# Masking and row maxima of a cross-attention block: one fused VectorE operation per head in place of an add and a maximum per bank

## The chip, the cores and the metric

The kernel runs on one core of a Trainium2 chip. Five engines work side by side, each with its own queue of instructions that it runs in order: TensorE (PE in the profile; PEld is its loading of weights), VectorE (DVE), ScalarE (ACT), GpSimd (POOL) and SyncE (SP, which issues most of the transfers). They wait for one another through semaphores. PE writes to the eight banks of PSUM, each 128 partitions by 512 fp32 columns; the other data lie in SBUF. The metric is the device time of one execution in microseconds (us).

## What is computed

A cross-attention block over 128 batch entries of 128 positions and 256 features, with 16 heads of 16 features. Queries come from `x`, keys and values from the context; position i may look at positions j < i only; the softmax runs over j; row 0 is set to zero. Then follow the output product, a residual and a layer norm, a feed-forward part of 1024 with ReLU, and a second residual and norm.

```
scores = jnp.einsum('bhqd,bhkd->bhqk', q, k) / jnp.sqrt(jnp.float32(D_K))
scores = jnp.where(j < i + mask, scores, NEG_INF)      # mask = 0
attn = jax.nn.softmax(scores, axis=-1).at[:, :, 0, :].set(0.0)
ctx = jnp.einsum('bhqk,bhkd->bhqd', attn, v)
x = layer_norm(query + ctx @ Wo + bo, ln1_g, ln1_b)
out = layer_norm(x + jax.nn.relu(x @ W1 + b1) @ W2 + b2, ln2_g, ln2_b)
```

## The kernel before

Two batch entries make a pair p, so there are 64 pairs, 0 to 63. The pairs are worked on in an overlapped way: in step p the scores and the softmax are those of pair p, the weighing with the values those of pair p-2, the hidden layer that of p-3, the second product that of p-4, and the projections prepare pair p+1. Steps 7 to 62 are regular: each consists of the same operations, and the order in which each engine gets them is written out by hand. For the middle steps that is the string `ORDER` (L1746), whose words are looked up in the table `OPS` (L1642) and called by `step` (L1761); the first regular steps and the last one have their words in calls of `do` written out one by one. An entry such as `w1-1` belongs to the step before. The pairs outside 7 to 62 use other functions (`mask`, `mask_high`, `maximum`, `low_maximum`), which stay as they are.

Because of the causal mask the query rows are split in halves. For the low rows (the first 64 positions of both entries, laid over 128 partitions) only 64 key columns matter; for the high rows 128. `scores_both` (matmuls at L440) writes the high scores of four heads to each of the banks 0 to 3 and the low scores of four heads to each of the banks 4 to 7. The constant `neg` holds 64 zeros and then a triangle with -1e30 above the diagonal.

Then, in the order of DVE's queue in a regular step: `maskA0` adds the triangle to the low scores of heads 0 to 3 and writes SBUF (tile `sm`, L464); `add3` adds it in place, in PSUM, to the second 64 columns of heads 12 to 15 (`mask_add`, L1552); `maskA1` (heads 4 to 7, L464) and `maskB` (heads 8 to 15, L456) do the rest of the low ones; `max3` takes the negated maxima of the high heads 12 to 15 out of bank 3 (`mask_max`, L1558); `lowmax` takes those of all 16 low heads out of `sm` (L920). `add1`, `max1`, `add2`, `max2`, `add0` and `max0` follow further down the step, between other work.

ACT makes the exponentials, one head at a time, with the sum over the row as a second result (`exponential_by_head`, L931): exp(score + nmx), where `nmx` is the negated maximum. `eh7` (high heads 14 and 15) is the first of a step, `el7` (low heads 14 and 15) the last. The high exponentials read PSUM, the low ones `sm`; both write `sm`. Three transposes on DVE (L533, `turn1`, `turn0`, `turn2`) take `sm` to `turned`, and transfers on SP's queue bring it to `brought` for the weighing two steps later.

The banks are shared. After the scores PE goes on with `v1` (a product for the values, bank 4), `o1` (output product, bank 5) and `q1` (queries, bank 7), all at L1147; they overwrite the banks of the low scores. `w1` (second product) uses bank 6, `k1` (keys) bank 3, and the products of the hidden layer (L1358) banks 0 to 2. The context (L612 and L617 on DVE) multiplies the weighed values by the inverse sums and stands in DVE's queue right before `maskA0`; it waits for the weighing on PE (L586, L596), which is the last that PE does before the scores. Between its products PE runs a few no-ops that are written into the order too.

Of the kernel before, what the change touches and what calls it, by code (L numbers as in the profile page):

```python
# [9 lines left out]
AF = mybir.ActivationFunctionType  # L10
ALU = mybir.AluOpType
AX = mybir.AxisListType

P = 128
NEG_INF = -1e30
# [4 lines left out]
def tile_cross_attention_block(  # L20
# [22 lines left out]
    nc = tc.nc  # L43
    B, S, D = x.shape
# [10 lines left out]
    HP = P // 2  # L55
# [18 lines left out]
    states = {}  # L74
# [103 lines left out]
    neg = const.tile([P, 2, HP], F32, tag="neg", name="neg")  # L178
# [67 lines left out]
    banks = psum.tile([P, 8, 512], F32, tag="banks", name="banks")  # L246
# [202 lines left out]
    def mask(p, hi, rs):  # L449
        st = states[p]  # L450
        n = P if hi else HP
        no = neg.rearrange("p u j -> p (u j)") if hi else neg[:, 1, :]
        if not hi and len(rs) == 2 and rs[0] and "both" in st:
            r = rs[0]
            at = 4 + r
            nc.vector.tensor_tensor(  # L456
                st["sm", 0][:, 4 * r : 4 * r + 8, :].rearrange("p (b n) j -> p b n j", b=2),
                banks[:, at : at + 2, : 4 * n].rearrange("p b (n j) -> p b n j", j=n),
                no[:, None, None, :].to_broadcast([P, 2, 4, n]),
                ALU.add,  # L460
            )
            return
        for r in rs:
            nc.vector.tensor_tensor(  # L464
                st["sm", hi][:, 4 * r : 4 * r + 4, :],
                st["sps", hi][r][:, : 4 * n].rearrange("p (n j) -> p n j", j=n),
                no[:, None, :].to_broadcast([P, 4, n]),
                ALU.add,
            )
# [448 lines left out]
    def low_maximum(p):  # L918
        st = states[p]
        nc.vector.tensor_reduce(st["nmx", 0], st["sm", 0], AX.X, ALU.max, negate=True)  # L920

    def exponential_by_head(p, hi, heads, summed=False):

        st = states[p]
        if summed and "su" not in st:
            st["su"] = small.tile([P, 2 * H], F32, tag="su", name=f"su_{p}")
        sm, nmx = st["sm", hi], st["nmx", hi]
        for h in heads:
            at = h % 4 // 2 * H + hi * HH + h // 4 * 2 + h % 2
            src = st["sps", 1][h // 4][:, h % 4 * P : h % 4 * P + P] if hi else sm[:, h, :]  # L930
            nc.scalar.activation(sm[:, h, :], src, AF.Exp, bias=nmx[:, h : h + 1], scale=1.0, **(  # L931
                {"accum_out": st["su"][:, at : at + 1]} if summed else {}
            ))

    hidden_all = const.tile([P, FC, TP], F32, tag="hT", name="hT")
    wt = const.tile([P, 4, FC // 2, P], F32, tag="wt", name="wt")
# [189 lines left out]
    class Seven:  # L1126
# [28 lines left out]
        b = property(lambda self: self.of(1))  # L1155
        f = property(lambda self: self.of(2))
# [270 lines left out]
    for which, first in (("c", c_first[:, 0:2]), ("x", tokens_of[0][:, 0:2])):  # L1427
        st = states[0]
# [27 lines left out]
    for m in range(KC):  # L1456
# [7 lines left out]
        for e in range(2):  # L1464
            if m == 0:
                nc.scalar.activation(
                    st["kT"][:, m, e, :], pk[:, :TP], AF.Identity,
                    bias=bkh[:, m, e : e + 1], scale=half[:, e : e + 1],
# [9 lines left out]
    for m in range(KC):  # L1478
# [7 lines left out]
        if m == 0:  # L1486
            nc.scalar.activation(
                st["qT"][:, m, :], pq[:, :TP], AF.Identity,
                bias=bqs_c[:, m : m + 1], scale=QSCALE,
# [8 lines left out]
    A, B = (0, 1), (2, 3)  # L1498
# [47 lines left out]
        }[n]  # L1546
        engine.tensor_tensor(c[:, n], left, right, how)  # L1547

    def mask_add(p, b):

        ps = banks[:, b].rearrange("p (n j) -> p n j", j=P)
        nc.vector.tensor_tensor(  # L1552
            ps[:, :, HP:], ps[:, :, HP:], neg[:, 1, None, :].to_broadcast([P, 4, HP]), ALU.add
        )

    def mask_max(p, b):

        nc.vector.tensor_reduce(  # L1558
            states[p]["nmx", 1][:, 4 * b : 4 * b + 4],
            banks[:, b].rearrange("p (n j) -> p n j", j=P), AX.X, ALU.max, negate=True,  # L1560
        )

    KINDS = {
        "V": (Values, 4), "O": (Attention, 5), "Q": (Queries, 7), "K": (Keys, 3),
# [16 lines left out]
    def means_of(p):  # L1581

        st = states[p]
        mv = st["mva"] = small.tile([P, 4, 2], F32, tag="mv", name=f"mv_{p}")
        bs = st.pop(("bs", p))
        for s in range(4):
            nc.vector.bn_aggr(mv[:, s], bs[:, s])
# [25 lines left out]
    def turn_x1_blocks(p):  # L1613
        nc.vector.transpose(
            x1_turned(p).rearrange("p j (u a) -> p u j a", a=32),
            states[p]["x1"].rearrange("p s (k j a) -> p (s k) j a", k=KC, a=32),
        )
# [20 lines left out]
    def bring_part(p, n):  # L1638
# [3 lines left out]
    OPS = {  # L1642
        "weigh": lambda p: weigh(p - 2),
        "scores": lambda p: scores_both(p),
        "context": lambda p: context(p - 2),
        "deviations": lambda p: scales_of(p),
        "means": lambda p: means_of(p),
        "stats1": lambda p: stats_of(p, p - 2, "t1", 0),
        "stats2": lambda p: stats_of(p, p - 6, "t2", 2),
        "norm1": lambda p: norm1(p - 2),  # L1650
# [2 lines left out]
        "finish2": lambda p: finish_shift(p - 6),  # L1653
        "store": lambda p: store(p - 6),
        "turnx": lambda p: turn_x1_blocks(p - 2),
        "maskA0": lambda p: mask(p, 0, (0,)),
        "maskA1": lambda p: mask(p, 0, (1,)),
        "maskB": lambda p: mask(p, 0, B),
        "lowmax": lambda p: low_maximum(p),
        "recip": lambda p: reciprocals(p),  # L1660
        "turni": lambda p: turn_inverse(p),
        "load": lambda p: load_ahead(p),
# [75 lines left out]
            p + 2, "xc", halves(states[p + 2]["xT"]), n  # L1738
        ) if p + 2 < NP else None
    for n in range(HH):  # L1740
        OPS[f"eh{n}"] = lambda p, n=n: exponential_by_head(p, 1, (2 * n, 2 * n + 1), True)
        OPS[f"el{n}"] = lambda p, n=n: exponential_by_head(p, 0, (2 * n, 2 * n + 1), True)
    for n in range(3):
        OPS[f"turn{n}"] = lambda p, n=n: turn(p, n < 2, n % 2)

# [1347 lines left out]
```

## Time and profile before

| | us |
|---|---|
| runs of the kernel | 1475.64, 1478.79, 1478.85 (median 1478.79) |
| span of the profiled execution, whose own time the page gives only as this span | 1476.0 |
| busy: PE / DVE / ACT / POOL over the span | 1450.0 / 1372.8 / 1304.3 / 1266.4 |
| one regular step (612 to 634 us is one) | 22.03 |
| exponentials on ACT: high, 944 of them, mean | 0.383 |
| exponentials on ACT: low, 944 of them, mean | 0.369 |

In the profile a row of a view in order of time gives start, duration, engine, line, operation, result and sources, and in brackets the idle time in front with what ended it. A row of a group gives line, engine, operation, names, shapes and count, then the busy time, the mean duration in ns, and the idle time in front with the releasers. A row of a table by stretches gives the stretch, its length, the busy time and count of each engine, the clock that PE was granted (1.00 is full), the share of the transfer engines and GB/s.

### The profile page before, as it was taken

How to read it: one execution, taken by the hardware profiler on the slowest of the kernel's cores; microseconds unless marked ns; L12 is line 12 of the kernel's file. 1: busy time of each engine (PE TensorE's matmuls, PEld its weight loads, DVE VectorE, ACT ScalarE, POOL GpSimd, SP SyncE). 2: the span in 40 equal slices, each digit the busy share in tenths (PEclk: the TensorE clock that was granted, in tenths of full speed). 3: DMA queues.
4: the chain of work that ended last, by engine and by line, in shares of the span. 5: the costliest groups of instructions: out<-in, count | busy, mean ns of one | idle time of the engine just before them, and what ended most of it. 6: DMA issues, size and time to landing. Idle time of an engine off the chain costs nothing.

```text
span 1476.0 us, 61938 instructions
## 1 busy us (share of the span) xinstructions
PE 1450.0 (98%) x20713; PEld 1394.3 (94%) x20713; DVE 1372.8 (93%) x3231; ACT 1304.3 (88%) x5559; POOL 1266.4 (86%) x1816
## 2 busy tenths in 40 slices
PE   8999899999999999999999999999999999999998
PEld 7778799999999999999999999999999999999988
DVE  6987999999999999999999999999999999999767
ACT  4659899999999999999999999999999999999743
POOL 5986898988988988988988988888898888887966
PEclk9999999999999999999999999999999999999999
DMA  8274766766766767776766766766776766774541
GB/s 202 66 142 104 178 162 149 159 152 156 167 158 155 154 152 157 169 159 152 165 147 151 166 157 157 163 149 153 163 160 157 161 147 154 163 163 113 130 109 51
DMA packets 367448, 220.33 MB, mean 149 GB/s; under 512 B 279600, under 2 KB 335152, under 8 KB 367152
## 3 DMA queue, kind: packets, MB, share of 16 engines
q1 hardware_dynamic: 364864, 214.27, 63.9%
q8 instruction: 187, 3.06, 0.9%
q10 hardware_dynamic: 2288, 2.11, 0.7%
q14 instruction: 109, 0.89, 0.2%
HBM read 55.06 MB, written 18.09 MB: 50 GB/s over the span
## 4 chain that ended last, share of the span: by engine, by line
PE 72%; ACT 7%; DVE 4%; DMA 3%; SPq 1%; POOL 1%; issue 1%; DVEq 0%; ACTq 0%; POOLq 0%
PE banks L1147 40%; PE banks L1358 20%; PE banks L440 5%; ACT sm L931 5%; PE banks L596 3%; DMA kT<-kr 2%; PE banks L586 2%; PE banks L971 1%; DMA brought<-turned 1%; ACT kr L1213 1%; PE banks L869 0%; PE banks L1044 0%; ACT qT L1175 0%; SPq L552 0%; PE banks L629 0%
## 5 line engine op out<-in xcount | busy, mean ns | idle before, releaser
L931 ACT ACTIVATE sm<-banks,nmx 128x128 f32<-128x128 f32 x944 | 336.8, 383 | 15.8 <-DVE nmx L1558 12.6
L931 ACT ACTIVATE sm<-sm,nmx 128x64 f32<-128x64 f32 x944 | 321.6, 369 | 1.4 <-DVE nmx L920 1.4
L533 DVE STREAM_TRANSPOSE turned<-sm 128x1024 f32<-128x1024 f32 x186 | 217.0, 1213 | 3.3 <-DMA brought<-turned 2.4
L931 ACT ACTIVATION_READ_ACCUMULATOR sm<-banks,nmx 128x1 f32 x944 | 211.4, 224 | 0.0
L931 ACT ACTIVATION_READ_ACCUMULATOR sm<-sm,nmx 128x1 f32 x944 | 207.8, 220 | 0.0
L1147 PE MATMUL banks<-wt,hS 128*128 128x128 f32 x1344 | 177.6, 275 | 0.0
L1358 PE MATMUL banks<-xS,w1t 128*128 128x128 f32 x1344 | 177.2, 275 | 0.0
L1147 PEld LDWEIGHTS banks<-wt,hS 128*128 128x128 f32 x1344 | 163.6, 192 | 0.1
L1358 PEld LDWEIGHTS banks<-xS,w1t 128*128 128x128 f32 x1344 | 163.4, 192 | 0.0
L1558 DVE TENSOR_REDUCE nmx<-banks 128x4 f32<-128x512 f32 x224 | 152.1, 679 | 1.9
L1547 POOL TENSOR_TENSOR hS<-hT 128x512 f32<-128x512 f32 x116 | 147.5, 1273 | 5.4 <-ACT hT L876 2.4
L1358 PE MATMUL banks<-brought,w 128*128 128x128 f32 x896 | 118.2, 275 | 0.0
L1608 POOL TENSOR_TENSOR x1b<-x,g_r 128x512 f32<-128x512 f32 x56 | 72.3, 1291 | 51.0 <-ACT x L703 51.0
L1147 PE MATMUL banks<-w,hT 128*128 128x128 f32 x896 | 109.8, 275 | 0.0
L1358 PEld LDWEIGHTS banks<-brought,w 128*128 128x128 f32 x896 | 109.0, 192 | 0.0
L440 PE MATMUL banks<-kT,qT 32*64 32x128 f32 (+1 forms) x3840 | 100.7, 331 | 6.3 <-DMA kT<-kr 3.7
L1147 PEld LDWEIGHTS banks<-w,hT 128*128 128x128 f32 x896 | 104.8, 192 | 0.1
L440 PEld LDWEIGHTS banks<-kT,qT 32*64 32x64 f32 x3840 | 82.7, 131 | 16.9 <-ACT hT L1399 4.9
L1534 POOL TENSOR_TENSOR oc<-cxT 128x128 f32<-128x128 f32 x112 | 49.0, 457 | 57.9 <-DVE cxT L617 56.9
L1387 ACT ACTIVATE hT<-hT,b1e_c 128x256 f32<-128x256 f32 x224 | 95.7, 509 | 1.2 <-DVE hT L1383 1.1
L1552 DVE TENSOR_TENSOR banks<-banks,neg 128x256 f32<-128x256 f32 x224 | 93.1, 416 | 0.0
L703 ACT ACTIVATE x<-t,nb,sd 128x256 f32<-128x256 f32 x126 | 68.4, 592 | 19.1 <-POOL nb L726 11.9
(322 smaller groups left out, 4841.1 us busy)
## 6 DMA issues: line engine op xcount, KB each, us to landing
brought<-turned SPq DMA_DIRECT2D x936, 128.0 KB, 2.4
out_dram<-t SPq DMA_DIRECT2D x63, 256.0 KB, 4.7
xb<-in_x_dram SPq DMA_DIRECT2D x124, 128.0 KB, 3.2
cb<-in_ctx_dram SPq DMA_DIRECT2D x124, 128.0 KB, 3.2
x<-in_x_dram SPq DMA_DIRECT2D x31, 512.0 KB, 5.4
kT<-kr SPq DMA_DIRECT2D x112, 128.0 KB, 2.7
brought<-turned SPq DMA_DIRECT2D x40, 96.0 KB, 2.2
w<-in_L_xattn_W_dram SPq DMA_DIRECT2D x2, 1024.0 KB, 7.8
```

Of the source, the lines that this page charges most:

```text
L440: nc.tensor.matmul(st["sps", hi][r][s * HP : (s + 1) * HP, m * 2 * n : (m + 1) * 2 * n].rearrange("p (e j) -> p e j", e=2), st["qT"][strip ...
L533: nc.vector.transpose(turned[:, :, at : at + 256].rearrange("p j (n a) -> p n j a", a=32), states[p]["sm", hi].rearrange("p h j -> p (h j) ...
L703: nc.scalar.activation(x1[:, s], t1[:, s], AF.Identity, bias=st["nb", 1][:, s], scale=sd[:, s])
L931: nc.scalar.activation(sm[:, h, :], src, AF.Exp, bias=nmx[:, h : h + 1], scale=1.0, **({"accum_out": st["su"][:, at : at + 1]} if summed e ...
L1147: nc.tensor.matmul(out, left(k) if self.depth > 1 else left, right(k) if self.depth > 1 else right, start=(n == 1 and k == 0), stop=(k == ...
L1358: nc.tensor.matmul(ps[:, i * P : (i + 1) * P].rearrange("p (n a) -> p n a", a=32), left(i), right, start=(n in (1, 2, 5) and i == 0), stop ...
L1387: nc.scalar.activation(self.hT[:, f, at], self.hT[:, f, at] if src is None else src, AF.Relu, bias=b1e_c[:, f : f + 1], scale=1.0,)
L1534: nc.gpsimd.tensor_tensor(c[:, n], left, right, how)
L1547: engine.tensor_tensor(c[:, n], left, right, how)
L1552: nc.vector.tensor_tensor(ps[:, :, HP:], ps[:, :, HP:], neg[:, 1, None, :].to_broadcast([P, 4, HP]), ALU.add)
L1558: nc.vector.tensor_reduce(states[p]["nmx", 1][:, 4 * b : 4 * b + 4], banks[:, b].rearrange("p (n j) -> p n j", j=P), AX.X, ALU.max, negate ...
L1608: nc.gpsimd.tensor_tensor(st["x1b"], st["x1b"] if n else st["x1"], (be1b_r if n else g1_r)[:, None, :].to_broadcast([P, 2, D]), ALU.add if ...
```

## The change

In the regular steps each head gets one DVE operation that adds the mask, multiplies by -1 and takes the minimum over the row: it reads the scores from PSUM and `neg` from SBUF, writes the negated masked scores to `sm`, and gives the minimum (the negated maximum) as a second result into `nmx`. The exponentials of these steps then read `sm` for both halves, with the factor -1 and `nmx` as before. The words of the order stay where they are: `maskA0`, `maskA1` and `maskB` do the low heads 0 to 3, 4 to 7 and 8 to 15; `lowmax` does nothing; `add`n does the first two high heads of bank n and `max`n the other two. All other steps keep their masks.

```
-    def exponential_by_head(p, hi, heads, summed=False):
+    def exponential_by_head(p, hi, heads, summed=False, negated=False):
...
-            nc.scalar.activation(sm[:, h, :], src, AF.Exp, bias=nmx[:, h : h + 1], scale=1.0, **(
-                {"accum_out": st["su"][:, at : at + 1]} if summed else {}
-            ))
+            if negated:
+                src = sm[:, h, :]
+            nc.scalar.activation(
+                sm[:, h, :], src, AF.Exp, bias=nmx[:, h : h + 1], scale=-1.0 if negated else 1.0,
+                **({"accum_out": st["su"][:, at : at + 1]} if summed else {}),
+            )
...
+    def negated(p, hi, h):
+
+        st = states[p]
+        n = P if hi else HP
+        no = neg.rearrange("p u j -> p (u j)") if hi else neg[:, 1, :]
+        nc.vector.tensor_tensor_reduce(
+            st["sm", hi][:, h, :], st["sps", hi][h // 4][:, h % 4 * n : h % 4 * n + n], no,
+            -1.0, -2 * NEG_INF, ALU.add, ALU.min, st["nmx", hi][:, h : h + 1],
+        )
+
+    def low_negated(p, heads):
+        for h in heads:
+            negated(p, 0, h)
+
     def mask_add(p, b):
-
-        ps = banks[:, b].rearrange("p (n j) -> p n j", j=P)
-        nc.vector.tensor_tensor(
-            ps[:, :, HP:], ps[:, :, HP:], neg[:, 1, None, :].to_broadcast([P, 4, HP]), ALU.add
-        )
+        for h in range(4 * b, 4 * b + 2):
+            negated(p, 1, h)
 
     def mask_max(p, b):
-
-        nc.vector.tensor_reduce(
-            states[p]["nmx", 1][:, 4 * b : 4 * b + 4],
-            banks[:, b].rearrange("p (n j) -> p n j", j=P), AX.X, ALU.max, negate=True,
-        )
+        for h in range(4 * b + 2, 4 * b + 4):
+            negated(p, 1, h)
...
-        "maskA0": lambda p: mask(p, 0, (0,)),
-        "maskA1": lambda p: mask(p, 0, (1,)),
-        "maskB": lambda p: mask(p, 0, B),
-        "lowmax": lambda p: low_maximum(p),
+        "maskA0": lambda p: low_negated(p, range(0, 4)),
+        "maskA1": lambda p: low_negated(p, range(4, 8)),
+        "maskB": lambda p: low_negated(p, range(8, 16)),
+        "lowmax": lambda p: None,
...
-        OPS[f"eh{n}"] = lambda p, n=n: exponential_by_head(p, 1, (2 * n, 2 * n + 1), True)
-        OPS[f"el{n}"] = lambda p, n=n: exponential_by_head(p, 0, (2 * n, 2 * n + 1), True)
+        OPS[f"eh{n}"] = lambda p, n=n: exponential_by_head(p, 1, (2 * n, 2 * n + 1), True, True)
+        OPS[f"el{n}"] = lambda p, n=n: exponential_by_head(p, 0, (2 * n, 2 * n + 1), True, True)
```

How that looks in DVE's queue, first before: from the end of the context of one regular step to the first operation behind the masks (`sm` is the tile of exponentials, `nmx` the negated maxima, `banks` PSUM).

```order
L612 TENSOR_TENSOR cxT<-banks,brought 128x8x32
L617 TENSOR_TENSOR cxT<-banks,brought 128x4x31
L617 TENSOR_TENSOR cxT<-banks,brought 128x4x32
L464 TENSOR_TENSOR sm_14760<-banks,neg 128x256
L1552 TENSOR_TENSOR banks<-banks,neg 128x4x64
L464 TENSOR_TENSOR sm_14760<-banks,neg 128x256
L456 TENSOR_TENSOR sm_14760<-banks,neg 128x512
L1558 TENSOR_REDUCE nmx_35_14762<-banks 128x4
L920 TENSOR_REDUCE nmx_35_14761<-sm_14760 128x16
L1293 TENSOR_TENSOR t_33_14820<-banks,x_13230 128x2x128
```

And after the change, in the same place of a regular step. The fused operation is printed as ISA with two results, and each is followed by a second instruction that writes one column of `nmx`. The lines left out are the further low heads and one high head in front, all of the same two forms.

```order
L617 TENSOR_TENSOR cxT<-banks,brought 128x4x31
L617 TENSOR_TENSOR cxT<-banks,brought 128x4x32
L1557 ISA sm_13899,nmx_32_13900<-banks,neg 128x64
L1557 ISA nmx_32_13900 128x1
...
L1557 ISA sm_13899,nmx_32_13901<-banks,neg 128x128
L1557 ISA nmx_32_13901 128x1
...
L1296 TENSOR_TENSOR t_30_13973<-banks,x_12782 128x2x128
L289 STREAM_TRANSPOSE cT_14020<-cb_13252 128x512
```

Six instructions have become 40: 16 low pairs and 4 high ones now stand between the context and the operation at L1293 (L1296 after the change). Further down the step each `add` and `max` becomes two high pairs in its old place.

ACT's queue, from the copies of the values to the low exponentials of one regular step, before (`vz` are the values, `qT` the queries, `su` the row sums):

```order
L1686 COPY vz_178<-banks 128x4x2x16
L1685 COPY vz_178<-banks 128x4x2x16
L931 ACTIVATE sm_14760,su_14836<-banks,nmx_35_14762 128x128 x2
L1175 ACTIVATE qT_14829<-banks,bqs_c 128x128 x2
L931 ACTIVATE sm_14760,su_14836<-banks,nmx_35_14762 128x128 x2
L1259 COPY vz_178<-banks 128x4x2x16
L931 ACTIVATE sm_14760,su_14836<-sm_14760,nmx_35_14761 128x64 x6
```

And after:

```order
L1697 COPY vz_178<-banks 128x4x2x16
L1696 COPY vz_178<-banks 128x4x2x16
L933 ACTIVATE sm_15320,su_15410<-sm_15320,nmx_35_15322 128x128 x2
L1178 ACTIVATE qT_15404<-banks,bqs_c 128x128 x2
L933 ACTIVATE sm_15320,su_15410<-sm_15320,nmx_35_15322 128x128 x2
L1262 COPY vz_178<-banks 128x4x2x16
L933 ACTIVATE sm_15320,su_15410<-sm_15320,nmx_35_15321 128x64 x6
```

The order is the same; the high exponentials read `sm` in place of the banks.

## Prediction

> **What bounds the kernel now.** The page first: which engine is full, and what the chain of waits runs through. Then two views of the regular step: the busy time of each engine in one step, and the rows of DVE, ACT and PE in order of time.
>
> ```profile
> span 1476.0 us, 61938 instructions
> PE 1450.0 (98%) x20713; PEld 1394.3 (94%) x20713; DVE 1372.8 (93%) x3231; ACT 1304.3 (88%) x5559; POOL 1266.4 (86%) x1816
> PE 72%; ACT 7%; DVE 4%; DMA 3%; SPq 1%; POOL 1%; issue 1%; DVEq 0%; ACTq 0%; POOLq 0%
> ```
>
> PE carries the chain. Busy PE is not proof of a bound, so the step itself is looked at. One step is the distance between two starts of the scores (L440), 22.03 us:
>
> ```profile
> core 0: us, PE busy (x) PEld busy (x) DVE busy (x) ACT busy (x) POOL busy (x), PEclk, DMA share, GB/s
> 608.94:630.97 22.03, 22.03 (x329) 21.59 (x329) 21.35 (x53) 20.89 (x93) 19.59 (x30) 1.00 0.65 145
> ```
>
> PE has no gap, but DVE has only 0.68 us of idle and ACT 1.14 us. Three engines are within about 5% of one another, so what a change on DVE costs depends on the loops between the engines. Here is DVE from the last transposes of one step to the masks of the next:
>
> ```profile
> 622.04 3.50 DVE L533 STREAM_TRANSPOSE turned<-sm 128x1024 f32<-128x1024 f32 x3
> 625.46 0.65 DVE L1377 TENSOR_TENSOR hT<-banks,hT 128x512 f32<-128x512 f32 x1
> ...
> 629.44 0.42 DVE L612 TENSOR_TENSOR cxT<-banks,brought 128x256 f32<-128x256 f32 x1
> 629.78 0.47 DVE L617 TENSOR_TENSOR cxT<-banks,brought 128x124 f32<-128x124 f32 x2
> 630.18 0.42 DVE L464 TENSOR_TENSOR sm<-banks,neg 128x256 f32<-128x256 f32 x1
> 630.52 0.42 DVE L1552 TENSOR_TENSOR banks<-banks,neg 128x256 f32<-128x256 f32 x1
> 630.85 0.41 DVE L464 TENSOR_TENSOR sm<-banks,neg 128x256 f32<-128x256 f32 x1
> 631.18 0.68 DVE L456 TENSOR_TENSOR sm<-banks,neg 128x512 f32<-128x512 f32 x1
> 631.78 0.68 DVE L1558 TENSOR_REDUCE nmx<-banks 128x4 f32<-128x512 f32 x1
> 632.38 1.21 DVE L920 TENSOR_REDUCE nmx<-sm 128x16 f32<-128x1024 f32 x1
> 633.50 0.41 DVE L1293 TENSOR_TENSOR t<-banks,x 128x256 f32<-128x256 f32 x1
> ```
>
> Records overlap: the one at 630.52 lasts 0.42 us, yet the next starts 0.33 us later. I price DVE by the distance of starts: 0.33 us for 256 columns, 0.60 for 512, 1.12 for 1024, that is 1.03 ns a column and about 0.065 us for each instruction. The masks stand at 630.18 to 632.38. Who waits for them stands in the rows of PE and ACT:
>
> ```profile
> 629.30 1.67 PE L440 MATMUL banks<-kT,qT 32*64 32x128 f32 x64
> 630.90 0.71 PE L1147 MATMUL banks<-wv,cT 128*128 128x128 f32 x4
> ...
> 631.67 0.61 PE L1147 MATMUL banks<-wo,cxT 128*128 128x128 f32 x4
> ...
> 632.34 0.61 PE L1147 MATMUL banks<-xT,wq 128*128 128x128 f32 x4
> ```
>
> ```profile
> 632.49 0.37 ACT L931 ACTIVATE sm<-banks,nmx 128x128 f32<-128x128 f32 x1 [0.19 <-DVE nmx L1558]
> ```
>
> PE's products after the scores (v1 at 630.90 in bank 4, o1 at 631.67 in bank 5, q1 at 632.34 in bank 7) overwrite the banks of the low scores. o1 needs the mask that ends at 631.26, q1 the one that ends at 631.86: 0.48 us to spare. ACT's first exponential (heads 14 and 15) starts at 632.49, and it waits for the maximum at 631.78. So the stretch from 630.18 on is in two loops, one through PE and one through ACT.
>
> **The ACT loop is already closed.** The exponentials of one step run without a gap from the first to the last, and the third transpose needs the last:
>
> ```profile
> 610.46 0.37 ACT L931 ACTIVATE sm<-banks,nmx 128x128 f32<-128x128 f32 x1 [0.18 <-DVE nmx L1558]
> 610.73 0.19 ACT L931 ACTIVATION_READ_ACCUMULATOR sm<-banks,nmx 128x1 f32 x1
> 610.82 0.36 ACT L931 ACTIVATE sm<-banks,nmx 128x128 f32<-128x128 f32 x1
> ...
> 623.66 0.35 ACT L931 ACTIVATE sm<-sm,nmx 128x64 f32<-128x64 f32 x1
> 623.90 0.21 ACT L931 ACTIVATION_READ_ACCUMULATOR sm<-sm,nmx 128x1 f32 x1
> ```
>
> From 610.46 to 624.11 are 13.65 us. The three transposes start 1.14 us apart ((3.50 - 1.21) / 2), so the third starts at 624.33, and from there DVE needs 5.85 us until its masks at 630.18. Masks to first exponential 2.31 + exponentials 13.65 + slack 0.22 + DVE 5.85 = 22.03 us: the whole step, with 0.2 us of slack.
>
> **What goes.** Per step on DVE: four adds of 256 columns (0.33 each), four maxima of 512 (0.60), two low masks of 256 (0.33), one of 512 (0.60) and the low maximum of 1024 (1.12): 1.32 + 2.40 + 0.66 + 0.60 + 1.12 = 6.10 us. Most of it stands beside PE's work; on the two loops are only the 1.67 us from the first mask to q1's bank and the 2.31 us to the first exponential.
>
> **What comes.** 32 fused operations, 16 of 64 columns and 16 of 128, each followed by an instruction that writes the accumulator to nmx, as the order shows. The trace has neither. The nearest rows for the fused operation are one with three operands and a constant at 128 columns, and the plain add at 128:
>
> ```profile
> 614.93 0.28 DVE L1262 TENSOR_TENSOR vz<-banks,vz 128x128 f32<-128x128 f32 x1
> 615.13 0.28 DVE L1293 TENSOR_TENSOR t<-banks,x 128x128 f32<-128x128 f32 x1
> ...
> 619.22 0.29 DVE L1188 SCALAR_TENSOR_TENSOR qT<-banks,qT 128x128 f32<-128x128 f32 x1
> 619.43 0.41 DVE L1193 SCALAR_TENSOR_TENSOR qT<-banks,qT 128x256 f32<-128x256 f32 x1
> ```
>
> Starts are 0.20 and 0.21 us apart. I take the second, 0.21 us, and 64 columns less for the low ones: 0.143 us. For the read the nearest is DVE's smallest operation, one column:
>
> ```profile
> 1470.36 0.15 DVE L1830 TENSOR_SCALAR sd_last<-mv_last 128x1 f32<-128x1 f32 x1
> 1470.43 0.47 DVE L1835 SCALAR_TENSOR_TENSOR t_last<-t_last,mv_last,g_r 128x256 f32<-128x256 f32 x1
> ```
>
> 0.07 us. ACT's own read of its accumulator (610.73 to 610.82) takes 0.09 us of its queue, so the value is of the right size. The pair is 0.213 us low and 0.28 us high. Bounds: from below, a read that costs nothing behind a plain add, 0.13 and 0.20 (nothing in the trace excludes that it is hidden); from above, a read that starts only when the record of the main operation ends, 0.22 + 0.07 and 0.29 + 0.07. I take the middle, since both instructions are of kinds whose neighbours overlap here.
>
> DVE's sum: 16 x 0.213 + 16 x 0.28 = 7.89 us for 6.10. Busy time goes from 21.35 to about 23.1 us, over the present step: DVE alone would make the step 0.8 to 1.1 us longer.
>
> **PE loop.** q1 now stands behind 16 low pairs and the two high ones that replace the first add: 16 x 0.213 + 2 x 0.28 = 3.97 us, with 0.1 for the tail of the last 4.07. It has 632.34 - 630.18 = 2.16 us. The start at 630.18 cannot move up, since the context in front (629.44) waits for PE's last product before the scores. So PE stands about 1.9 us at o1 and q1 in each step.
>
> **ACT loop.** The first exponential stands behind those pairs and the two high ones in the place of the maximum: 16 x 0.213 + 4 x 0.28 + 0.1 = 4.63 us for 2.31, so 2.32 us later. The 16 high exponentials read SBUF instead of PSUM. Two groups of 256 columns with the same function show what that is worth:
>
> ```profile
> L1387 ACT ACTIVATE hT<-hT,b1e_c 128x256 f32<-128x256 f32 x224 | 95.7, 509 | 1.2 <-DVE hT L1383 1.1
> L1399 ACT ACTIVATE hT<-banks,b1e_c 128x256 f32<-128x256 f32 x168 | 67.6, 472 | 12.0 <-DVE hT L1397 12.0
> ```
>
> ```profile
> L931 ACT ACTIVATE sm<-banks,nmx 128x128 f32<-128x128 f32 x944 | 336.8, 383 | 15.8 <-DVE nmx L1558 12.6
> ```
>
> 37 ns each on top of 383, 0.59 us per step, all of it between the first exponential and the third transpose. The factor -1 instead of 1 is a field of the same instruction: nothing. Less the slack of 0.19 us (0.03 for the signal), the loop grows by 2.32 + 0.59 - 0.19 = 2.7 us, the longest of the three, and the step becomes 24.7 us. The high banks are now freed by DVE and not by the exponentials; PE's wait for them is not in its rows, so that is worth nothing. Queued behind the waiting o1 and q1 are all of PE's later products, among them the weighing that DVE's context waits for; behind ACT's first exponential stand the copies of the queries, keys and hidden rows, which PE and DVE wait for later; behind a late DVE its transposes and the context. All move with the step, none adds to it.
>
> **Sum.** 56 steps x 2.72 = 152 us on the span of 1476.0, so 1628. The runs shown have a median of 1478.79, 2.8 above that span: **1631 us**.
>
> **The rivals.**
> 1. *PE loop alone.* If ACT finds the 0.8 us back (an exponential from SBUF at no more than from PSUM, or slack that the rows don't show), the step grows by 1.95 us: 109 us, 1588. For it: ACT has 1.14 us of idle per step; against: none of it lies between the first and last exponential.
> 2. *The read is hidden.* 16 x 0.13 + 4 x 0.20 + 0.1 = 2.98 us to the first exponential, 0.67 later; with 0.59 - 0.19 the loop grows by 1.07: 60 us, 1539.
> 3. *The read waits for the pipe.* Pairs of 0.29 and 0.36: 6.18 us, 3.87 later, growth 4.27: 239 us, 1718. Plain neighbours overlap by 0.09 us, which speaks against it; but this one reads what the instruction in front has just made, and no row has that. The Trainium skill, "VectorE: DVE Perf Modes", section "The DRAIN you can't avoid", states that no operation begins before the pipe of the one ahead is empty. By that rule this rival would hold; the overlap at 630.52 (0.42 us long, the next 0.33 us later) disagrees with it for plain operations.
> 4. *Faster.* The fused form streams 3072 columns for 5120. If a pair cost only its columns, 0.067 and 0.133 us, the first exponential would come 0.6 us earlier. The point is where 16 low and 4 high pairs take 2.31 - 0.1 - 0.4 = 1.8 us: 0.08 and 0.13 a pair. Even then PE keeps its 22.03 us; only the stage of first regular steps, where PE is not full, could gain, some 5 us: 1474.
>
> ```profile
> 150.00:172.00 22.00, 16.74 (x263) 15.01 (x264) 20.20 (x48) 20.22 (x105) 16.88 (x27) 1.00 0.69 179
> ```
>
> Against it stands every short DVE row here: none starts its successor in less than 0.065 us beyond its columns.
> 5. *Not as named.* If the reads don't reach the chip as instructions, it is case 2.
>
> **How the numbers follow.** Forecast 0.50; PE loop alone 0.15; read hidden 0.12; read waits for the pipe 0.13; still longer pairs (both records in full, 0.37 and 0.44, over 1720) 0.05; no change 0.03; faster 0.02. The range from case 2 to case 3, 1538 to 1720, leaves out about 0.1 and is no wider than the bounds of the pair. A measurement of this kernel tells 0.3% (4.4 us) from no change: faster 0.02, within 0.03, slower 0.95.
>
> **What would show it.** In the profile after: the distance of starts of the fused rows (0.14 and 0.21, their reads 0.07); PE idle before o1 and q1 behind the fused line, some 2.5 us a step; ACT's wait before its first exponential from 0.19 to some 2 us; the high exponentials at about 420 ns instead of 383; the scores 24.7 us apart. Wrong would be: pairs under 0.1 us, or a step bound by DVE with PE's wait in another place, such as the transposes.

## The result, and the profile after

| | before | after |
|---|---|---|
| runs of the kernel, median (lowest to highest), us | 1478.40 (1475.64 to 1478.85) | 1533.05 (1531.56 to 1533.62) |
| span of the profiled execution, us | 1476.0 | 1530.8 |
| one regular step, us | 22.03 | 23.07 |

The ratio is 1.0375, 95% interval 1.036 to 1.039: slower, by 55 us. The prediction said slower, but 1631, and its range began at 1538; the time is 5 us below it. First the page after, where the chain of waits has moved from PE to ACT and DVE:

```profile
span 1530.8 us, 64847 instructions
PE 1488.6 (97%) x20713; PEld 1404.7 (92%) x20713; DVE 1344.9 (88%) x6143; ACT 1330.5 (87%) x5559; POOL 1268.4 (83%) x1816
ACT 45%; DVE 27%; PE 7%; issue 4%; DMA 3%; SPq 1%; POOL 1%; DVEq 0%; POOLq 0%; ACTq 0%
```

DVE's busy time fell (1372.8 to 1344.9) although the kernel became slower. The view of one step gives the same: DVE 20.81 us busy where it was 21.35.

```profile
651.00:674.07 23.07, 22.79 (x343) 21.83 (x332) 20.81 (x105) 21.34 (x94) 19.66 (x29) 1.00 0.71 162
```

DVE in order of time, from the first pair of a step to the first operation behind the pairs:

```profile
651.26 0.23 DVE L1557 CUSTOM_DVE_ANT_0 sm<-banks,neg 128x64 f32<-128x64 f32 x1
651.41 0.08 DVE L1557 DVE_READ_ACCUMULATOR2_ANT nmx<- 128x1 f32 x1
651.41 0.22 DVE L1557 CUSTOM_DVE_ANT_0 sm<-banks,neg 128x64 f32<-128x64 f32 x1
651.56 0.08 DVE L1557 DVE_READ_ACCUMULATOR2_ANT nmx<- 128x1 f32 x1
...
651.85 0.28 DVE L1557 CUSTOM_DVE_ANT_0 sm<-banks,neg 128x128 f32<-128x128 f32 x1
652.06 0.08 DVE L1557 DVE_READ_ACCUMULATOR2_ANT nmx<- 128x1 f32 x1
652.06 0.28 DVE L1557 CUSTOM_DVE_ANT_0 sm<-banks,neg 128x128 f32<-128x128 f32 x1
...
654.00 0.28 DVE L1557 CUSTOM_DVE_ANT_0 sm<-banks,neg 128x128 f32<-128x128 f32 x1
654.21 0.08 DVE L1557 DVE_READ_ACCUMULATOR2_ANT nmx<- 128x1 f32 x1
654.21 0.28 DVE L1557 CUSTOM_DVE_ANT_0 sm<-banks,neg 128x128 f32<-128x128 f32 x1
654.42 0.08 DVE L1557 DVE_READ_ACCUMULATOR2_ANT nmx<- 128x1 f32 x1
654.42 0.42 DVE L1296 TENSOR_TENSOR t<-banks,x 128x256 f32<-128x256 f32 x1
```

The read and the next fused operation start at the same moment (651.41 both, 652.06 both): a read has a record of 0.08 us but takes nothing of the queue. A pair is 0.145 us for 64 columns (twelve heads from 652.27 to 654.00 are 1.73) and 0.21 for 128, about what the fused operation alone was taken to cost. Who waits for the pairs stands in PE's and ACT's rows of the same step:

```profile
650.35 1.67 PE L440 MATMUL banks<-kT,qT 32*64 32x128 f32 x64
...
654.14 0.71 PE L1150 MATMUL banks<-xT,wq 128*128 128x128 f32 x4 [0.22 <-DVE nmx L1557]
```

```profile
654.33 0.40 ACT L933 ACTIVATE sm<-sm,nmx 128x128 f32<-128x128 f32 x1 [0.90 <-DVE nmx L1557]
654.64 0.19 ACT L933 ACTIVATION_READ_ACCUMULATOR sm<-sm,nmx 128x1 f32 x1
654.73 0.39 ACT L933 ACTIVATE sm<-sm,nmx 128x128 f32<-128x128 f32 x1
...
668.09 0.37 ACT L933 ACTIVATE sm<-sm,nmx 128x64 f32<-128x64 f32 x1
668.42 0.60 ACT L1377 COPY hT<-banks 128x512 f32<-128x512 f32 x1
```

And DVE at the end of the exponentials and at the next step's first pair:

```profile
668.58 1.25 DVE L533 STREAM_TRANSPOSE turned<-sm 128x1024 f32<-128x1024 f32 x1 [0.29 <-ACT sm L933]
...
674.33 0.23 DVE L1557 CUSTOM_DVE_ANT_0 sm<-banks,neg 128x64 f32<-128x64 f32 x1
```

The first exponential waits 0.90 us for its maximum, and the third transpose now waits 0.29 us for the last exponential: the ACT loop has no slack left. Its terms, before and after:

| us per step | predicted change | before | after | change |
|---|---|---|---|---|
| first mask to first exponential | +2.32 | 2.31 | 3.07 (651.26 to 654.33) | +0.76 |
| first exponential to the end of the last | +0.59 | 13.65 | 14.22 (to 668.55) | +0.57 |
| slack, then the signal to DVE | -0.19 | 0.22 | 0.03 | -0.19 |
| third transpose to the next first mask | 0 | 5.85 | 5.75 (668.58 to 674.33) | -0.10 |
| sum | +2.72 | 22.03 | 23.07 | +1.04 |

The end of the last exponential is the start of the last (668.09), the 0.33 us by which low ones follow one another, and 0.13 for the rest of its read. 56 steps by 1.04 are 58 us; the spans differ by 54.8, since some steps were over 22.03 before already. PE's q1 starts 3.79 us after the scores where it was 3.04 (632.34 - 629.30). PE's loop alone would give 22.03 + 0.75 = 22.78, 0.29 less than ACT's.

### The profile page after: what moved, and what is told of

The parts are those of the page before. It is cut to its first block, busy times and chain, and to the rows that moved or that the text cites. A ratio compares the mean times of both kernels' runs of the same rounds, so it can differ in the third digit from the quotient of the medians.

```text
span 1530.8 us, 64847 instructions
## 1 busy us (share of the span) xinstructions
PE 1488.6 (97%) x20713; PEld 1404.7 (92%) x20713; DVE 1344.9 (88%) x6143; ACT 1330.5 (87%) x5559; POOL 1268.4 (83%) x1816
## 3 DMA queue, kind: packets, MB, share of 16 engines
q14 instruction: 131, 1.07, 0.2%
## 4 chain that ended last, share of the span: by engine, by line
ACT 45%; DVE 27%; PE 7%; issue 4%; DMA 3%; SPq 1%; POOL 1%; DVEq 0%; POOLq 0%; ACTq 0%
ACT sm L933 37%; DVE sm L1557 8%; PE banks L1150 3%; ACT kr L1216 3%; DVE hT L1380 2%; DVE turned L533 2%; DVE turned L1625 2%; DMA brought<-turned 2%; DVE banks L1383 2%; DVE hT L1386 2%; ACT qT L1178 2%; ACT hT L1371 2%; ACT hT L1374 2%; PE banks L1361 2%; DVE hT L1400 2%
## 5 line engine op out<-in xcount | busy, mean ns | idle before, releaser
L933 ACT ACTIVATE sm<-sm,nmx 128x64 f32<-128x64 f32 (+1 forms) x1840 | 667.0, 378 | 50.0 <-DVE nmx L1557 48.7
L933 ACT ACTIVATION_READ_ACCUMULATOR sm<-sm,nmx 128x1 f32 x1840 | 375.0, 204 | 0.0
L1557 DVE CUSTOM_DVE_ANT_0 sm<-banks,neg 128x128 f32<-128x128 f32 (+1 forms) x1792 | 333.8, 251 | 3.2 <-PE banks L440 1.6
L533 DVE STREAM_TRANSPOSE turned<-sm 128x1024 f32<-128x1024 f32 x186 | 223.3, 1227 | 18.9 <-ACT sm L933 15.4
L1557 DVE DVE_READ_ACCUMULATOR2_ANT nmx<- 128x1 f32 x1792 | 148.8, 83 | 0.2 <-issue 0.2
L1296 DVE TENSOR_TENSOR t<-banks,x1b 128x256 f32<-128x256 f32 x168 | 53.1, 316 | 108.8 <-POOL cc L1537 62.5
L1590 DVE BATCH_NORM_STATS2 bsa<-t 128x6 f32<-128x256 f32 x224 | 83.2, 414 | 0.0
```

The lines of the kernel that those rows point to most:

```text
L533: nc.vector.transpose(turned[:, :, at : at + 256].rearrange("p j (n a) -> p n j a", a=32), states[p]["sm", hi].rearrange("p h j -> p (h j) ...
L1296: nc.vector.tensor_tensor(to, src, of, ALU.add)
L1557: nc.vector.tensor_tensor_reduce(st["sm", hi][:, h, :], st["sps", hi][h // 4][:, h % 4 * n : h % 4 * n + n], no, -1.0, -2 * NEG_INF, ALU.a ...
L1590: nc.vector.bn_stats(states[p]["bs", p][:, at + s], states[q][t][:, s])
```

## The experiments

All keep the steps outside 7 to 62 as they are; a change of the order is made in the 52 steps that the string `ORDER` writes. All are compared with the kernel before. A step is the distance between two starts of the scores in the regular part of each trace.

**Which half costs it?** Two kernels do one half each. The first keeps the old masks, maximum and exponentials for the low heads:

```
-        "maskA0": lambda p: low_negated(p, range(0, 4)),
...
-        "lowmax": lambda p: None,
+        "maskA0": lambda p: mask(p, 0, (0,)),
...
+        "lowmax": lambda p: low_maximum(p),
...
```

> Only the high heads are fused; the low masks and the low maximum are those of before. Theory of two loops (ACT loop: masks to first exponential + exponentials + third transpose to the next masks; PE loop: masks of the low banks to q1): first exponential 0.33+0.42+0.33+0.60+0.42+0.12 = 2.2 us after the first mask (2.31 before, 3.07 after the change), exponentials 14.2 (SBUF), rest 5.8: step 22.2, so some 11 us over before, 1489. Rival 'only PE's wait for the low banks counts': they are freed as before, 1478. Rival 'DVE's load counts': DVE has less work than before, 1478 or less.

The second keeps the add, the maximum and the exponentials out of PSUM for the high heads:

```
     def mask_add(p, b):
-        for h in range(4 * b, 4 * b + 2):
-            negated(p, 1, h)
+        ps = banks[:, b].rearrange("p (n j) -> p n j", j=P)
+        nc.vector.tensor_tensor(
+            ps[:, :, HP:], ps[:, :, HP:], neg[:, 1, None, :].to_broadcast([P, 4, HP]), ALU.add
+        )
...
```

> Only the low heads are fused; the high add, maximum and exponentials from PSUM are those of before. Two loops: q1's bank is free 16 x 0.145 + 0.33 + 0.1 = 2.75 us after the first mask instead of 1.68, PE loop 22.7; first exponential 2.65 + 0.68 + 0.05 = 3.4, ACT loop 3.4 + 13.65 + 5.8 = 22.8: 1521. Rival 'the exponentials' reading of SBUF is most of the cost': close to before, under 1490.

High alone: 1486.4 us, 1.0084 (1.0062 to 1.0106), step 22.22. Low alone: 1524.12, 1.0345 (1.0324 to 1.0367), step 22.93. Both are within about 3 us of what the two loops gave. ACT with only the high heads fused, then with only the low ones:

```profile
658.15 0.27 ACT L1697 COPY vz<-banks 128x128 f32<-128x128 f32 x1 [0.71 <-PE banks L1150]
658.31 0.27 ACT L1696 COPY vz<-banks 128x128 f32<-128x128 f32 x1
658.47 0.41 ACT L933 ACTIVATE sm<-sm,nmx 128x128 f32<-128x128 f32 x1
```

```profile
653.38 0.37 ACT L933 ACTIVATE sm<-banks,nmx 128x128 f32<-128x128 f32 x1 [1.20 <-DVE nmx L1575]
```

In the first there is no wait for the maximum any more: the exponential follows the copies of the values, 2.02 us behind the first mask. What remains, 0.19 us a step, comes from the stretch of the exponentials (14.47 us from the first to the end of the last, 0.24 of it a wait of the queries' copy for q1). In the second the first one waits 1.20 us. So nearly all of the cost comes from the low half, and it is a matter of what stands in front of the first exponential (and of q1, as the next experiment shows): 16 low pairs of 0.145 are 2.32 us where two low masks of 0.33 and one of 0.60 were 1.26, so +1.06. The low maximum of 1.12 us that the change removes stood behind the maximum that the first exponential waits for, and its time comes back only as idle time: in the changed kernel VectorE stands for 2.26 us of a step (23.07 - 20.81), before for 0.68. The high pairs give a part of it back: three of them and the last read are 0.63 + 0.08 us, where an add of 0.33 and the whole maximum of 0.68 stood, so -0.30. Together that is the +0.76 measured.

**Which loop binds?** The pairs of heads 14 and 15 go ahead of `maskA1` and `maskB`, so that ACT can begin early while q1's bank comes free later.

```
-        ro0-2 br1 maskA0 ro2-2 add3 oc0 ro1-2 v1 maskA1 oc2 maskB hs0-1 o1 max3 vk1 vk0 q1
+        ro0-2 br1 maskA0 ro2-2 add3 max3 oc0 ro1-2 v1 maskA1 oc2 maskB hs0-1 o1 vk1 vk0 q1
```

> As changed, but in the 52 steps of the order string the high heads 14 and 15 stand before the low heads 4 to 15, so the first exponential comes 1.5 us earlier and q1's bank 0.42 us later. Two loops: ACT loop 21.6, PE loop 22.78 + 0.42 = 23.2, slower than as changed: about 1540. Rival 'ACT loop alone': down to before, under 1490.

1553.18 us, 1.0539 (1.0518 to 1.0559), step 23.49. ACT in one step:

```profile
660.09 0.41 ACT L933 ACTIVATE sm<-sm,nmx 128x128 f32<-128x128 f32 x1
660.39 0.20 ACT L933 ACTIVATION_READ_ACCUMULATOR sm<-sm,nmx 128x1 f32 x1
660.48 0.40 ACT L933 ACTIVATE sm<-sm,nmx 128x128 f32<-128x128 f32 x1
660.77 0.20 ACT L933 ACTIVATION_READ_ACCUMULATOR sm<-sm,nmx 128x1 f32 x1
662.30 0.63 ACT L1178 ACTIVATE qT<-banks,bqs_c 128x128 f32<-128x128 f32 x2 [1.33 <-PE banks L1150]
```

The first exponential no longer waits, so with the ACT loop alone the kernel would have become faster; that rival falls. But the copy of the queries, the third thing in ACT's order, waits 1.33 us for q1, with 30 exponentials behind it. PE's q1 here, and the same copy in the changed kernel:

```profile
661.33 0.71 PE L1150 MATMUL banks<-xT,wq 128*128 128x128 f32 x4 [0.22 <-DVE nmx L1557]
```

```profile
655.12 0.62 ACT L1178 ACTIVATE qT<-banks,bqs_c 128x128 f32<-128x128 f32 x2
```

The size expected was 23.2, from PE's loop by itself. What counts is a joined path: from the masks through q1 to the copy, and from there through the exponentials. q1 starts 3.30 us behind the first mask (658.03), 0.42 more than in the changed kernel, and the step is 0.42 longer than there (23.49 for 23.07). The copy that waits starts 0.97 us after q1 (662.30 - 661.33); in the changed kernel it starts 0.98 us after it (655.12 - 654.14), so there the joined path is within 0.01 us of the one through the first exponential. The same low pairs delay both, and by these sums a shorter way to the first exponential alone would not shorten the step.

**Is it VectorE's sum of work, or the place of the work?** Two kernels were to add some 0.64 us of work, once in a gap of DVE and once ahead of the first exponential, as eight small adds:

```
+        for _ in range(8):
+            nc.vector.tensor_tensor(spare, neg[:, 0, :16], neg[:, 1, :16], ALU.add)
```

> As changed, plus eight small DVE operations (16 columns, some 0.08 us each, 0.64 us in all, result unused) in 52 steps, placed where DVE waits 1.22 us for PE and POOL behind the high heads of bank 2. Two loops: nothing, 1533. Rival 'the load of DVE sets the step': 0.64 x 52 = 33 us more, 1566.

> The same eight small operations, placed between the last low head and the high heads 14 and 15. Two loops: behind q1's bank, but in the ACT loop: 0.64 x 52 = 33 us more, 1566. Rival 'only PE's wait for the low banks counts': 1533.

Both miss by far: 1750.31 us, 1.185 (step 27.3), and 1809.03, 1.2255 (steps of 27.9 to 29.3). TensorE's granted clock, 0.999 in the changed kernel, is 0.946 and 0.933 in these two. The adds did not last what was assumed. The group of the first kernel, and of the second:

```profile
L1578 DVE TENSOR_TENSOR spare<-neg 128x16 f32<-128x16 f32 x416 | 225.3, 542 | 12.5
```

```profile
L1578 DVE TENSOR_TENSOR spare<-neg 128x16 f32<-128x16 f32 x416 | 199.6, 480 | 12.5
```

Half a microsecond for 16 columns on average; single ones took 0.17 to 1.30 us. Two things were new in them. All eight write the same tile, so that in the order as built each waits for the one ahead; and both sources lie in SBUF, while GpSimd's operations there (up to 1.3 us long) ran beside them. The rows tell the two causes apart. From the second kernel, an add, the GpSimd operation beside it, and a later add of the same eight with no GpSimd operation beside it:

```profile
759.68 1.19 DVE L1578 TENSOR_TENSOR spare<-neg 128x16 f32<-128x16 f32 x1
759.56 1.28 POOL L1550 TENSOR_TENSOR hS<-hS,hT 128x512 f32<-128x512 f32 x1
762.55 0.17 DVE L1578 TENSOR_TENSOR spare<-neg 128x16 f32<-128x16 f32 x1
```

In the two kernels 264 adds had no GpSimd operation beside them, and all of these lasted 0.17 to 0.18 us, although all but five of them wait for the one ahead. All 208 adds that lasted over 1 us ended 0.03 to 0.04 us after a GpSimd operation did. So the wait makes an add 0.21 us from start to start where 0.08 was assumed, and GpSimd beside it makes the rest. The Trainium skill, "SBUF — State Buffer", section "Who interferes with whom", states that a VectorE operation with two SBUF inputs contends with a GpSimd operation that reads SBUF; the trace agrees, with 1.19 us in place of 0.17. As tests of the load these runs say nothing, so they were made again from the pair itself, whose price is known and which has one SBUF source (pairs beside a GpSimd addition of 1.28 us, at 656.70 in the first of the next two kernels, still follow one another after 0.21 to 0.22 us): three high heads are done a second time, in the same two places (8, 9 and 8 in the gap, 12, 13 and 12 ahead).

```
+    def extra(p, heads):
+        for h in heads:
+            negated(p, 1, h)
...
+        "extra": lambda p: extra(p, (8, 9, 8)),
...
-        add1 el4 w5-1 max1 br3 el0 add2 o2 cc0 wk-1 eh3 k1 finish1-1 vb ok2 va eh2 q2 stats2 o3
+        add1 el4 w5-1 max1 br3 el0 add2 o2 cc0 extra wk-1 eh3 k1 finish1-1 vb ok2 va eh2 q2 stats2 o3
```

> As the changed kernel, but in 52 of the steps the fused operation of heads 8, 9 and 8 is issued once more, with the same result, in the place where VectorE otherwise waits 1.22 us for GpSimd (line 1296, released by cc of line 1537). Three more pairs of 0.21 us are 0.63 us of VectorE's time per step. Two-loops theory (what counts is when VectorE frees q1's bank and gives the first exponential its maximum): nothing is added, 1530 to 1538 us. Rival, VectorE's sum of work sets the step: 52 x 0.63 = 33 us more, about 1566.

```
+        "extra": lambda p: extra(p, (12, 13, 12)),
...
-        ro0-2 br1 maskA0 ro2-2 add3 oc0 ro1-2 v1 maskA1 oc2 maskB hs0-1 o1 max3 vk1 vk0 q1
+        ro0-2 br1 maskA0 ro2-2 add3 oc0 ro1-2 v1 maskA1 oc2 maskB hs0-1 o1 extra max3 vk1 vk0 q1
```

> As the changed kernel, but in 52 of the steps the fused operation of heads 12, 13 and 12 is issued once more between the last low head and heads 14 and 15: behind the pair that frees q1's bank, ahead of the pair that the first exponential waits for. ACT-loop theory: 0.63 us more in each step, 52 x 0.63 = 33 us, about 1566 (step 23.7). Rival, only TensorE's wait for q1's bank counts: unchanged, about 1533.

In the gap: 1532.62 us, 1.0376 (1.0353 to 1.0399), step 23.07, as the changed kernel. Ahead: 1562.23, 1.058 (1.0563 to 1.0596), step 23.69 to 23.71, +0.63. The operation that waits for GpSimd in the changed kernel, and in the kernel with work in that gap:

```profile
658.52 0.42 DVE L1296 TENSOR_TENSOR t<-banks,x1b 128x256 f32<-128x256 f32 x1 [1.22 <-POOL cc L1537]
```

```profile
659.23 0.42 DVE L1296 TENSOR_TENSOR t<-banks,x1b 128x256 f32<-128x256 f32 x1 [0.58 <-POOL cc L1537]
```

The wait shrinks by what was put in, and the step stays, as the two loops gave it. In the other kernel q1 does not move (3.79 us behind the scores, 665.68 - 661.89), and the first exponential does (4.62 us behind them, where it was 3.98):

```profile
661.89 1.67 PE L440 MATMUL banks<-kT,qT 32*64 32x128 f32 x64
665.68 0.71 PE L1150 MATMUL banks<-xT,wq 128*128 128x128 f32 x4 [0.22 <-DVE nmx L1557]
```

```profile
666.51 0.40 ACT L933 ACTIVATE sm<-sm,nmx 128x128 f32<-128x128 f32 x1 [1.53 <-DVE nmx L1557]
```

So DVE's sum of work does not set the step of the changed kernel; the place ahead of the first exponential does, one for one, while PE's waits stay as they are.

**What do the exponentials out of SBUF cost?** Two kernels write the result of the high heads back into its bank, where the exponentials then read it: one with all heads fused, one with the high heads alone.

```
-            if negated:
+            if negated and not hi:
                 src = sm[:, h, :]
...
+        scores_of = st["sps", hi][h // 4][:, h % 4 * n : h % 4 * n + n]
...
-            st["sm", hi][:, h, :], st["sps", hi][h // 4][:, h % 4 * n : h % 4 * n + n], no,
+            scores_of if hi else st["sm", hi][:, h, :], scores_of, no,
```

> As changed, but the high fused operation writes its result back to its bank, and the high exponentials read PSUM with factor -1. Two loops: the ACT loop falls by 0.57 to 22.5, the PE loop stays at 22.78 and now sets the step: about 1519. Rival 'ACT loop alone': 22.5, 1504. Rival 'the SBUF source of the exponentials costs nothing': 1533 as changed.

> Low masks as before; high heads fused with the result in the bank, high exponentials from PSUM with factor -1. Two loops: first exponential 2.2 us after the first mask, exponentials 13.65: ACT loop 21.7, PE loop 22.03 as before, so PE sets the step again: 1475 to 1479, no change or a few us faster where single steps were longer than 22.03 before. Rival 'any fused form costs, by its number of instructions': over 1485.

Both miss: 1543.3 us, 1.0468 (1.0443 to 1.0492), step 23.25; and 1517.4, 1.0274 (1.0258 to 1.0289), step 22.76. The exponentials did get faster (in the first, the 32 of a step and what lies between take 13.59 us, from 660.85 to 674.44, for 14.22), but the pairs got slower. DVE of the first kernel:

```profile
657.73 0.29 DVE L1558 CUSTOM_DVE_ANT_0 banks<-banks,neg 128x128 f32<-128x128 f32 x1
657.94 0.14 DVE L1558 DVE_READ_ACCUMULATOR2_ANT nmx<- 128x1 f32 x1
658.12 0.30 DVE L1558 CUSTOM_DVE_ANT_0 banks<-banks,neg 128x128 f32<-128x128 f32 x1
658.33 0.14 DVE L1558 DVE_READ_ACCUMULATOR2_ANT nmx<- 128x1 f32 x1
658.33 0.22 DVE L1558 CUSTOM_DVE_ANT_0 sm<-banks,neg 128x64 f32<-128x64 f32 x1
```

The first pair takes 0.39 us until the next, the second 0.21. The order as built tells the two apart:

```
L1558 ISA banks,nmx_12_4421<-banks,neg 128x128 [waits DVE_49]
L1558 ISA nmx_12_4421 128x1
L1558 ISA banks,nmx_12_4421<-banks,neg 128x128
L1558 ISA nmx_12_4421 128x1
```

A pair that writes the bank that the pair just ahead wrote has a wait on VectorE's own semaphore; the first one of another bank has none. ACT's exponential of head 14 waits in the same way until head 15 is done too (it starts at 660.85; the read of head 15 ends at 660.81, that of head 14 at 660.42). With all heads fused it is the ACT loop again that is closed: the third transpose starts right behind the read of the last exponential.

```profile
674.15 0.29 ACT L933 ACTIVATION_READ_ACCUMULATOR sm<-sm,nmx 128x1 f32 x1
674.48 1.25 DVE L533 STREAM_TRANSPOSE turned<-sm 128x1024 f32<-128x1024 f32 x1
```

From the first mask (657.14) to the first exponential 3.71 us, exponentials 13.59, signal 0.04, third transpose to the next first mask (680.39) 5.91: 23.25, the step. The 3.71 are 0.64 more than in the changed kernel, which takes back the 0.63 that the exponentials gain; the other 0.17 lie almost all behind the third transpose. With the high heads alone the first exponential comes 2.64 us after the first mask (647.01 - 644.37), where 2.2 was expected. If that wait is the cause, and not PSUM as the place of the result, pairs of one bank only have to stand apart. That was tried in the kernel with the high heads alone, in its 52 steps of the string `ORDER`; `n`h is the pair of head h.

```
-        ro0-2 br1 maskA0 ro2-2 add3 oc0 ro1-2 v1 maskA1 oc2 maskB hs0-1 o1 max3 vk1 vk0 q1
+        ro0-2 br1 maskA0 ro2-2 n12 oc0 ro1-2 v1 maskA1 n13 oc2 maskB hs0-1 o1 n14 n15 vk1 vk0 q1
...
-        add1 el4 w5-1 max1 br3 el0 add2 o2 cc0 wk-1 eh3 k1 finish1-1 vb ok2 va eh2 q2 stats2 o3
-        cc2 kk w6-1 max2 cc1 el6 add0 hs2-1 br2 h1-1 vf el2 ob oa max0 w3-1 qk2 cc3 eh5 xs0-1
+        n6 n8 el4 w5-1 n4 n9 br3 el0 n7 n10 n5 o2 cc0 wk-1 eh3 k1 finish1-1 vb ok2 va eh2 q2 stats2 o3
+        cc2 kk w6-1 n0 n11 cc1 el6 n1 hs2-1 br2 h1-1 vf el2 ob oa n2 n3 w3-1 qk2 cc3 eh5 xs0-1
```

> As the kernel with only the high heads fused and their results in their banks (1517.4 us, step 22.76), but in 52 steps no high pair follows another of its bank where it can be helped: heads 12 and 13 stand behind the low masks of heads 0 to 3 and 4 to 7, and the pairs of banks 1 and 2 alternate. Theory, the 0.39 us of a pair in its bank is a wait for the pair just ahead in the same bank, not the price of writing PSUM: pairs that are apart take 0.21 us, the first exponential comes 2.35 us after the first mask, the exponentials take 13.65, and the ACT loop is 21.8, below TensorE's 22.03: step 22.0 to 22.2, 1475 to 1485 us. Rival, a result in PSUM makes the pair cost 0.39 us wherever it stands: step near 22.76 as in the run ahead, 1510 us or more.

1492.52 us, 1.0104 (1.0088 to 1.0121), step 22.29: far from the rival's 22.76, and 0.1 us (7.5 us in all) above the upper end of what was expected. DVE, and ACT a little later:

```profile
642.05 0.33 DVE L1558 CUSTOM_DVE_ANT_0 banks<-banks,neg 128x128 f32<-128x128 f32 x1
642.29 0.14 DVE L1558 DVE_READ_ACCUMULATOR2_ANT nmx<- 128x1 f32 x1
642.29 0.33 DVE L1558 CUSTOM_DVE_ANT_0 banks<-banks,neg 128x128 f32<-128x128 f32 x1
```

```profile
643.71 0.37 ACT L933 ACTIVATE sm<-banks,nmx 128x128 f32<-128x128 f32 x1 [0.19 <-DVE nmx L1558]
```

The pairs follow one another after 0.24 to 0.25 us, and the read again costs the queue nothing. What is left of the loss is a wait that this order itself made: head 6 is due before the last pair of its bank (head 5) is over. So that bank was moved forward:

```
-        lowmax eh7 oc1 v2 br0 xs2-1 qk w1-1 hs1-1 ok eh6 tokc-1 w2-1 tokx vk2 el3 oc3 hs3-1 v3
-        n6 n8 el4 w5-1 n4 n9 br3 el0 n7 n10 n5 o2 cc0 wk-1 eh3 k1 finish1-1 vb ok2 va eh2 q2 stats2 o3
+        lowmax eh7 oc1 v2 br0 xs2-1 qk w1-1 hs1-1 ok eh6 n6 tokc-1 w2-1 n4 tokx vk2 el3 oc3 hs3-1 v3
+        n7 n8 el4 w5-1 n5 n9 br3 el0 n10 o2 cc0 wk-1 eh3 k1 finish1-1 vb ok2 va eh2 q2 stats2 o3
```

> As the run ahead (pairs of a bank apart, 1492.5 us, step 22.29), but heads 4 and 6 move up beside the two transposes at L289 and heads 5 and 7 one place forward, so that the last pair of bank 1 is over before the exponential of head 6 is due (it waited 0.33 us there). Theory: with that wait gone the ACT loop is 21.9 to 22.0 and TensorE sets the step again: 22.03 to 22.1, about 1480 us with the four steps that keep the old sequence (0.7 us each). Rival, the slower step comes from VectorE's greater work with the pairs, not from that wait: step 22.29, 1492.

1480.03 us, 1.0023 (1.0012 to 1.0033), regular step 22.03. The chain of that kernel:

```profile
PE 70%; DVE 12%; ACT 9%; DMA 4%; issue 1%; SPq 1%; POOL 1%; DVEq 0%; ACTq 0%; POOLq 0%
```

PE sets the step again, as in the kernel before. Together the two runs show that with the high heads alone the wait between pairs of one bank was the cause of the loss, and that exponentials that read PSUM, with the maximum in time, cost the step nothing. Pairs of one bank set apart were not tried with all heads fused; the low pairs stay out of this version, and none of the kernels is faster than the one before: PE is full at 22.03.

## Why the prediction was wrong, point by point

- **The step that failed** is the price of the pair, in "What comes": the read was taken at 0.07 us of DVE's queue, from the smallest DVE operation, and the pair at 0.213 and 0.28. Measured: 0.145 and 0.21. The fused operation was priced right (0.143 and 0.21); its read is hidden. That is 16 x 0.068 + 3 x 0.07 = 1.30 us of the 1.68 us per step that the forecast is off (2.72 forecast, 1.04 measured). A further 0.28 is a pair too many: the first exponential needs head 14 only (it starts at 654.33, before the read of head 15 at 654.42), so three high pairs stand ahead of it and not four. The last 0.10 is DVE's stretch to the next masks, which became a little shorter.
- **Rival 2, "the read is hidden", is what happened.** It gave 1.07 us of growth where 1.04 came, and 1539 us. Its prices were 0.13 and 0.20, a plain add's, and its count of high pairs was one too high; the two errors nearly cancel (2.98 us to the first exponential, 3.07 measured), and DVE's shorter stretch, which it did not have, takes the rest. That its total came so near is partly luck. The forecast took the middle between "hidden" and "waits for the pipe" because neighbours of both kinds overlap, but these neighbours overlap by the whole read.
- **Rival 3, "the read waits for the pipe",** fell: it asked for 0.29 and 0.36 a pair. The rule of the Trainium skill that stands beside it ("VectorE: DVE Perf Modes", "The DRAIN you can't avoid") has an exception in the same section, which the prediction left out: a next operation that is not held starts earlier. The trace agrees with the exception: the read begins 0.15 us after the start of an operation whose record lasts 0.23.
- **The ACT loop as the bound** was right, and its other terms too: +0.57 for the exponentials out of SBUF (0.59 predicted; the high ones went from 383 to 403 ns, but the distance of the first two from 0.36 to 0.40 us, 654.33 to 654.73), and the slack of 0.19 used up. The last in-bank kernel, with the exponentials back at PSUM and the maximum in time (1480.03), agrees. What the prediction did not see is the second path into the same loop, through q1 and the copy of the queries: it says of that copy that it moves with the step and adds nothing, which holds here by 0.01 us only.
- **PE loop:** right as a mechanism, 0.75 us instead of 1.91 (4.07 - 2.16; the rival writes 1.95), from the same price. By itself it stays 0.29 us below the ACT loop. "PE idle some 2.5 us before o1 and q1" was wrong: 0.22 us before q1 in a step, and in the rows of PE's weight loads 0.21, 0.26 and 0.41 us ahead of v1, o1 and q1.
- **DVE's load:** predicted 23.1 us in a step, measured 20.81. It does not bind; shown by the 0.63 us in the gap that cost nothing.
- **Sum and bounds:** "56 steps" held. The lower end of the range, 1538, was rival 2; the time lies 5 us below because the step grew by 1.04 and not 1.07 us (some 2 us) and some steps had been longer than 22.03 already (some 3 us).

## What to carry to other kernels

When a fused operation replaces an operation over many heads and a later reduction, add up what stands ahead of the first consumer, before and after: here the fused form takes less of VectorE in all, but it moves the reduction of all 16 low heads from behind the first exponential to the front of it. Look too for a second consumer that the same work holds up, as q1 and its copy here. Price a second instruction that only writes out an accumulator by the distance of starts and not by its record, and keep "hidden" as a forecast of its own where neighbouring records overlap. Before a result is put elsewhere, look in the built order for new waits: two neighbouring pairs that write one bank cost 0.17 to 0.18 us each time, until they stood apart.

## What the runs showed of the hardware that was not expected

- The read of the accumulator (83 ns mean, 1792 of them) starts together with the next fused operation and costs nothing between them:

```profile
L1557 DVE DVE_READ_ACCUMULATOR2_ANT nmx<- 128x1 f32 x1792 | 148.8, 83 | 0.2 <-issue 0.2
```

The Trainium skill, "VectorE: DVE Perf Modes", section "Two Vector instructions with no wait between them", counts such an operation as two instructions, the main one and an accumulator read, and judges for each by itself whether it is held; the trace has two records for each operation, and neither is held, at 0.145 us a pair of 64 columns.
- With the result in PSUM the read's record is 0.14 us instead of 0.08, and pairs without a wait follow after 0.21 to 0.25 us.
- Adds of 16 columns with both sources in SBUF lasted 0.17 to 0.18 us with no GpSimd operation beside them and up to 1.30 us with one; each of the 208 over 1 us ended within 0.04 us of a GpSimd operation's end. The pairs, with one source in PSUM, kept their 0.21 us beside it.
